# Moving PSUM copies of `ht` and `v` from VectorE to ScalarE in a two-layer graph network kernel

## The chip, the cores and the metric

The kernel runs on one core of one Trainium2 chip, as a single launch. The metric is device time in microseconds (us), as a median of several runs. A lower number is better. All data is float32.

## What is computed

The input `x` has 16 graphs of 1024 nodes and 256 channels; all graphs share one 1024 x 1024 adjacency matrix `adj`. Two layers follow each other, both with a layer norm and a ReLU ahead and a residual around them. Cut to what matters:

```python
# layer 0
h = max(layernorm(x), 0)
fea = h.transpose(0, 2, 1)                       # channels x nodes
diff = c_adj[:, None, :] - c_adj[:, :, None]     # c_adj: mean of h over channels
A_s = 2 * abs(abs(sigmoid(diff) - 0.5) - 0.5)    # symmetric
g = relu((fea @ (adj * A_s)) * para)             # the queries
k, v = split(h @ kv_w)                           # keys, values
x = x + softmax(q @ k.T * scale) @ v             # 4 heads of 64
# layer 1
h = max(layernorm(x), 0)
y = relu(batchnorm((A_hat @ h) @ W1.T + b1))     # A_hat: normalised adj + eye
x = x + batchnorm(y @ W2.T + b2)
```

The batch norms need statistics over all 16 graphs, so the second half of layer 1 starts only after the first half of the last graph.

## The kernel before

**Stages.** A short start prepares graph 0 (layer norm, transposes, keys, values, weights of the adjacency, queries). Then `attention()` runs over the graphs. While the attention of graph b is computed, a stream of smaller pieces called the background does other work: queries (`queries`), keys and values (`keys_values`) of graph b+1, the second layer norm and the product with the normalised adjacency for graph b-1 (`normed`, `aggregate`), the product with W1 for graph b-1 (`hidden`), and the layer norm and transposes for graph b+2 (`summed`, `prepare`). In the trace one graph takes about 146.75 us from about 192 us on. After the last graph, `second()` does the rest of layer 1.

**Order.** There is no automatic scheduling: the code issues instructions in the order in which it runs, and each engine executes its own list in that order. The list of one graph is 16 steps of attention (2 channel halves x 2 node halves x 4 pairs of key tiles). Each step issues two score products (line 882), their `exp` on ScalarE (line 890), one or more background pieces, and the products with the values for the step before (line 923). Background pieces have a cost in microseconds, and a piece is taken as long as the sum is behind its due value. `soon(...)` puts an action off to the next piece.

**The two places that the change touches.** `transposed(b, k)` turns the layer norm's output `h_a` (nodes x channels) into `ht` (channels x nodes): four TensorE transposes (line 396) fill one PSUM tile `htp` of 128 x 512, and one copy (line 399) brings it to SBUF. Two such tiles make one `ht`, and two `ht` one graph. `keys_values(b)` computes keys (`pk`, copied by ScalarE at line 624) and then values in four groups g: 16 matmul instructions fill one PSUM tile `pv`, and two copies of 128 x 256 (line 641) bring it to the two `v` tiles.

**PSUM tiles.** All these products take their tile from one pool with two buffers:

```python
ps_mm = st.enter_context(tc.tile_pool(name=f"ps_mm_{kind}", bufs=2, space=PSUM))
def bank(name):
    return ps_mm.tile([P, FB], F32, tag="mm", name=name)
```

So the third tile in a row can be written only when the first has been emptied: `pv` group 2 waits for the copies of group 0, and the product after a pair of `htp` tiles waits for the copy of the first of them. The score tiles `sc` have two buffers of their own, which `exp` empties.

**What stands around these copies.** On VectorE: the sums of the softmax (`acc`, lines 909 and 912), turning and folding them (lines 940 and 941), the weighting with `adj` (line 437), differences of the weights (line 512), combinations of the queries' products (lines 520 to 546), the scaling by `para` (line 498), statistics of the layer norms (line 317) and of the batch norm (line 741). On ScalarE: `exp` (line 890), `abs` and `tanh` for the weights (lines 450 and 458), ReLU of the queries (line 500, which waits for line 498) and of the layer norms (line 341), the copies of `o` (line 932) and of the first products (lines 515, 516, 673), and the bias for `y` (line 737).

Of the kernel before, what the change touches and what calls it, by code (L numbers as in the profile page):

```python
# [23 lines left out]
def gnn_two_layers_kernel(  # L24
# [12 lines left out]
    nc = tc.nc  # L37
# [6 lines left out]
    FB = 512  # L44
# [51 lines left out]
    def layers(shifted):  # L96
# [67 lines left out]
        def bank(name):  # L164
            return ps_mm.tile([P, FB], F32, tag="mm", name=name)

        def product(dst, left, right, start, stop):

            for e in range(2):
                r = slice(e * HW, (e + 1) * HW)  # L170
                nc.tensor.matmul(dst[r], left[:, r], right, start=start, stop=stop)  # L171
# [213 lines left out]
        def transposed(b, k, halves=range(NH)):  # L385

            h = hs["a", b]
            if 0 in halves:
                ht = p3.tile([P, N], F32, tag="ht", name=f"ht_{b}_{k}")
                hts.setdefault(b, []).append(ht)  # L390
            ht = hts[b][k]
            for g in halves:
                pt = bank(f"htp_{b}_{k}_{g}")
                for j in range(FB // P):
                    t = g * (FB // P) + j
                    nc.tensor.transpose(
                        pt[:, j * P : (j + 1) * P], h[:, t, k * P : (k + 1) * P], ident
                    )
                nc.vector.tensor_copy(ht[:, g * FB : (g + 1) * FB], pt)  # L399

        def differences(b):

# [210 lines left out]
        def keys_values(b):  # L613
            ht = hts[b]
            ks[b] = [p4.tile([P, N], F32, tag="k", name=f"k_{b}_{k}") for k in range(CC)]
            for g in range(NH):
                for j in range(CC):
                    cols = slice(g * FB, (g + 1) * FB)
                    pk = bank(f"pk_{b}_{j}_{g}")
                    for k in range(CC):  # L620
                        product(
                            pk, kvw[:, k, j * P : (j + 1) * P], ht[k][:, cols], k == 0, k == CC - 1
                        )
                    nc.scalar.copy(ks[b][j][:, cols], pk)  # L624
                    yield 1.71

            vs[b] = [p4.tile([P, NT, P], F32, tag="v", name=f"v_{b}_{k}") for k in range(CC)]
            for g in range(NT // 2):
                pv = bank(f"pv_{b}_{g}").rearrange("p (j c) -> p j c", j=2)
                for j in range(2):  # L630
                    t = 2 * g + j
                    for k in range(CC):
                        product(
                            pv[:, j, :],
                            ht[k][:, t * P : (t + 1) * P],
                            kvw[:, k, C : 2 * C],
                            k == 0,
                            k == CC - 1,
                        )
                for k in range(CC):  # L640
                    nc.vector.tensor_copy(  # L641
                        vs[b][k][:, 2 * g : 2 * g + 2, :], pv[:, :, k * P : (k + 1) * P]
                    )
                yield 1.71
# [127 lines left out]
        def prepare(b, products):  # L772


            yield from islice(products, 1)
            w = weighers[b]
            for k in range(CC):
                yield from weave(islice(products, 3), (0, islice(w, AHEAD // 2)))
                yield TOP
                transposed(b, k)  # L780
                yield 1.0
            yield from products
# [3 lines left out]
        def background(b):  # L786

            if b == 0:
                differences(1)
                for k in range(CC):  # L790
                    yield TOP
                    transposed(1, k)
                    yield 1.0
                w, products, norm = weighers[1], keys_values(1), Norm(2, True).all()
                yield from weave(
                    islice(products, 4), (0, double(islice(w, 8))), (0, islice(norm, 4))
                )
                yield from weave(
                    plain_queries(1), (0, norm), (0, w), (5, graph()), (7, degrees())
                )  # L800
                differences(2)
                yield from islice(products, 2)
                yield from prepare(2, products)
                return
            before = hidden(b - 1)
            gather = aggregate(b - 1)
            if b + 1 < B:
                w, products, norm = weighers[b + 1], keys_values(b + 1), normed(b - 1)
                yield from weave(islice(products, 4), (0, islice(w, 4)))
                if b == 1:  # L810
                    load_later()
                yield from weave(queries(b + 1), (0, double(w)), (9, islice(norm, 5)))
                yield next(gather)
                yield from weave(products, (0, norm))
            else:
                yield from weave(endings.pop(), (2, normed(b - 1)))
                yield next(gather)
# [240 lines left out]
        with st:  # L1058
            if shifted:
                for b in range(B):  # L1060
                    if b > 0:
                        load_x(b)
                    run(Norm(b, True).all())
                    differences(b)
                    for k in range(CC):
                        transposed(b, k)
                    run(islice(weighers[b], AHEAD))
                    run(weave(plain_queries(b), (0, weighers[b])))
                    if b == 0:
                        run(degrees(), graph())  # L1070
                        load_later()
                    run(keys_values(b))
                    shifted_attention(b)
                    norm = Norm(b, False)
                    run(norm.all())
                    nc.gpsimd.dma_start(out=x1_d[b], in_=xs[b])
                    if b == B - 1:
                        attn.close()
                        turns.append(second(kind))
                    run(aggregate(b), hidden(b))  # L1080
# [351 lines left out]
```

## Time and profile before

| | |
|---|---|
| median of three runs | 2658.61 us (2658.59 to 2659.17) |
| the profiled execution's own time | 2658.52 us |
| its span in the trace | 2656.6 us |
| TensorE (PE) matmuls busy | 2550.8 us, 96% of the span |
| VectorE (DVE) busy | 1904.3 us, 72% |
| ScalarE (ACT) busy | 1402.4 us, 53% |
| copies `ht<-htp` on VectorE, line 399 | 64 of 128x512, 40.6 us together |
| copies `v<-pv` on VectorE, line 641 | 128 of 128x256, 48.1 us together |

Busy time of an engine is the sum of its instructions in the trace. A matmul's busy time gets longer when the granted clock of TensorE is lower. A line of the waits names who waited, and which instruction ended the wait. A line of the timeline gives the start, the length, the engine, the line of the kernel, what is written and read, and in brackets the idle time of the engine just before, with what ended it. Times are counted from the start of the span.

### The profile page before, as it was taken

How to read it: one execution, taken by the hardware profiler on the slowest of the kernel's cores; microseconds unless marked ns; L12 is line 12 of the kernel's file. 1: busy time of each engine (PE TensorE's matmuls, PEld its weight loads, DVE VectorE, ACT ScalarE, POOL GpSimd, SP SyncE). 2: the span in 40 equal slices, each digit the busy share in tenths (PEclk: the TensorE clock that was granted, in tenths of full speed). 3: DMA queues.
4: the chain of work that ended last, by engine and by line, in shares of the span. 5: the costliest groups of instructions: out<-in, count | busy, mean ns of one | idle time of the engine just before them, and what ended most of it. 6: DMA issues, size and time to landing. Idle time of an engine off the chain costs nothing.

```text
span 2656.6 us, 31371 instructions
## 1 busy us (share of the span) xinstructions
PE 2550.8 (96%) x11626; PEld 948.2 (36%) x11626; DVE 1904.3 (72%) x3029; ACT 1402.4 (53%) x1841; POOL 391.4 (15%) x456
## 2 busy tenths in 40 slices
PE   8999999999999999999999999999999999989995
PEld 3333333333333333333333333333333333334443
DVE  5678686868777676868677686778686776657675
ACT  5774555646373645546463736455464734335544
POOL 1640001000000001000000000010000001026653
PEclk9999999999999999999999999999999999999997
DMA  4554333142524333341525243332415242355459
GB/s 165 182 180 170 100 107 136 59 175 72 178 83 148 105 138 100 103 140 58 184 76 178 80 151 99 132 111 95 144 60 183 80 147 103 112 189 211 185 188 368
DMA packets 131041, 363.45 MB, mean 137 GB/s; under 512 B 15424, under 2 KB 32320, under 8 KB 124736
## 3 DMA queue, kind: packets, MB, share of 16 engines
q1 hardware_dynamic: 110272, 282.70, 31.4%
q0 software_dynamic: 20608, 78.66, 7.8%
q8 instruction: 94, 1.54, 0.3%
q14 instruction: 67, 0.55, 0.1%
HBM read 286.79 MB, written 74.51 MB: 136 GB/s over the span
## 4 chain that ended last, share of the span: by engine, by line
PE 63%; DVE 21%; ACT 8%; issue 3%; DMA 2%; POOL 1%; SPq 0%; POOLq 0%; DVEq 0%; ACTq 0%
PE pa L171 14%; PE sc L882 12%; PE o L923 11%; PE m_f L1227 7%; PE py L171 7%; DVE acc L912 5%; PE pk L171 4%; ACT w L450 4%; DVE w L512 3%; PE pv L171 3%; PE pg L171 2%; DMA out_dram<-xo_f 2%; DVE w L437 2%; DVE st_b L317 1%; ACT w L458 1%
## 5 line engine op out<-in xcount | busy, mean ns | idle before, releaser
L890 ACT ACTIVATE p<-sc 128x1024 f32<-128x1024 f32 x512 | 494.8, 1019 | 484.3 <-PE sc L882 483.9
L912 DVE TENSOR_TENSOR acc<-acc,p 128x1024 f32<-128x1024 f32 x384 | 471.5, 1228 | 113.5 <-ACT p L890 92.2
L882 PE MATMUL sc<-q,k 64*128 64x512 f32 x2048 | 511.6, 618 | 3.3 <-ACT p L890 3.2
L923 PE MATMUL o<-p,v 128*64 128x512 f32 x2048 | 496.6, 606 | 0.0
L171 PE MATMUL pg<-w,h_a 128*64 128x512 f32 x1600 | 358.1, 592 | 3.7 <-ACT k L624 1.9
L171 PE MATMUL pa<-aht,h_b 128*64 128x512 f32 x1536 | 344.8, 593 | 3.5 <-ACT h_b L341 3.4
L882 PEld LDWEIGHTS sc<-q,k 64*128 64x128 f32 x2048 | 177.1, 187 | 330.2 <-issue 291.7
L450 ACT ACTIVATE w<-cbc,csum 128x512 f32<-128x512 f32 x256 | 293.7, 1199 | 0.0
L171 PE MATMUL py<-at,w 128*64 128x512 f32 x1024 | 232.3, 596 | 3.6 <-DVE ht L399 3.6
L437 DVE SCALAR_TENSOR_TENSOR w<-w,adj 128x1024 f32<-128x1024 f32 x128 | 159.6, 1247 | 78.3 <-ACT w L458 74.2
L923 PEld LDWEIGHTS o<-p,v 128*64 128x64 f32 x2048 | 124.3, 136 | 251.5 <-issue 248.4
L171 PEld LDWEIGHTS pg<-w,h_a 128*64 128x64 f32 x1600 | 115.5, 137 | 231.9 <-issue 213.7
L171 PEld LDWEIGHTS pa<-aht,h_b 128*64 128x64 f32 x1536 | 110.8, 137 | 216.9 <-issue 207.2
L738 POOL DMA_DIRECT2D y_d<-y x128 | 70.5, 551 | 788.9 <-ACT y L737 781.0
L737 ACT ACTIVATE y<-py,vec 128x512 f32<-128x512 f32 x128 | 87.5, 684 | 160.0 <-PE py L171 137.4
L171 PE MATMUL pv<-kvw_f,ht 128*64 128x256 f32 x1024 | 138.2, 424 | 34.0 <-DVE v L641 34.0
L458 ACT ACTIVATE w<-w 128x1024 f32<-128x1024 f32 x128 | 135.1, 1055 | 1.8
L741 DVE BATCH_NORM_STATS2 stats<-y 128x6 f32<-128x512 f32 x128 | 85.7, 688 | 69.7 <-ACT y L737 69.6
L512 DVE TENSOR_TENSOR w<-w,w 128x1024 f32<-128x1024 f32 x112 | 132.8, 1217 | 1.5
L93 POOL TENSOR_SCALAR lnsm_b<-mv_b 128x4 f32<-128x4 f32 x32 | 12.1, 379 | 793.4 <-DVE mv_b L319 793.4
L171 PEld LDWEIGHTS py<-at,w 128*64 128x64 f32 x1024 | 73.4, 138 | 153.8 <-issue 133.7
L341 ACT ACTIVATE h_b<-x,lnsm_b 128x256 f32<-128x256 f32 x128 | 67.8, 591 | 110.7 <-DVE lnsm_b L330 110.7
(155 smaller groups left out, 2806.9 us busy)
## 6 DMA issues: line engine op xcount, KB each, us to landing
aht<-aht_d SPq DMA_DIRECT2D x224, 512.0 KB, 5.6
adj<-in_adj_dram SPq DMA_DIRECT2D x128, 512.0 KB, 4.6
y_d<-y POOLq DMA_DIRECT2D x128, 256.0 KB, 2.6
yin_f<-y_d SPq DMA_DIRECT2D x32, 1024.0 KB, 6.3
x<-in_x_dram SPq DMA_DIRECT2D x32, 512.0 KB, 5.0
para<-in_para_dram SPq DMA_DIRECT2D x64, 256.0 KB, 3.9
x_d<-x POOLq DMA_DIRECT2D x16, 1024.0 KB, 10.4
xo_f<-x_d SPq DMA_DIRECT2D x32, 512.0 KB, 8.2
```

Source lines behind the costliest of these rows:

```text
L171: nc.tensor.matmul(dst[r], left[:, r], right, start=start, stop=stop)
L437: nc.vector.scalar_tensor_tensor(w, w, 1.0, a, op0=ALU.add, op1=ALU.mult)
L450: nc.scalar.activation(w[:, t, :].rearrange("p (t q) -> p t q", q=P), cbc[:, q * NT // NH : (q + 1) * NT // NH], AF.Abs, bias=csum[:, th * ...
L458: nc.scalar.activation(made[i], made[i], AF.Tanh, scale=-0.5 / C)
L512: nc.vector.tensor_sub(block(i)[part], block(x)[part], block(y)[part])
L737: nc.scalar.activation(y, made, AF.Identity, bias=b1[:, j : j + 1])
L741: nc.vector.bn_stats(stats1[:, j, i, :], y)
L882: nc.tensor.matmul(sc[:, e, :], ks[b][k][r, m * P : (m + 1) * P], qs[b][k][r, f * FB : (f + 1) * FB], start=True, stop=True,)
L890: nc.scalar.activation(pr, sc, AF.Exp)
L912: nc.vector.tensor_add(self.acc, self.acc, pr)
L923: nc.tensor.matmul(self.o[r, :], vs[b][k][:, m, r], pr[:, e, :], start=(m == 0), stop=(m == NT - 1),)
L1227: nc.tensor.matmul(made, left[:, j, :], right[:, j, :], start=(j == 0), stop=(j == JH - 1))
```

## The change

Both copies are issued on ScalarE in place of VectorE. Nothing else is edited: the places in the code, the tiles and their shapes stay. Since each engine's list follows the order of the code, each copy now stands in ScalarE's list at the point where the code reaches it.

```diff
@@ transposed @@
                     nc.tensor.transpose(
                         pt[:, j * P : (j + 1) * P], h[:, t, k * P : (k + 1) * P], ident
                     )
-                nc.vector.tensor_copy(ht[:, g * FB : (g + 1) * FB], pt)
+                nc.scalar.copy(ht[:, g * FB : (g + 1) * FB], pt)
@@ keys_values @@
                 for k in range(CC):
-                    nc.vector.tensor_copy(
+                    nc.scalar.copy(
                         vs[b][k][:, 2 * g : 2 * g + 2, :], pv[:, :, k * P : (k + 1) * P]
                     )
                 yield 1.71
```

## The prediction

> **What bounds the kernel now.** I read the busy shares first, then the waits of TensorE (PE), then the timeline around the longest of them, then the granted clock there.
>
> ```profile
> PE 2550.8 (96%) x11626; PEld 948.2 (36%) x11626; DVE 1904.3 (72%) x3029; ACT 1402.4 (53%) x1841; POOL 391.4 (15%) x456
> PE pv L171 <- DVE v L641: 34.0, 14, 2.6
> PE py L171 <- DVE ht L399: 3.6, 13, 0.3
> 1113.64 3.62 PE L171 MATMUL pv<-kvw_f,ht 128*64 128x256 f32 x32
> 1119.85 3.63 PE L171 MATMUL pv<-kvw_f,ht 128*64 128x256 f32 x16 [2.58 <-DVE v L641]
> 1127.44 1.90 PE L171 MATMUL pv<-kvw_f,ht 128*64 128x256 f32 x16
> ...
> core 0: us, PE busy (x), PEclk, DMA share, GB/s
> 1117.30:1119.80 2.50, 0.00 (x0) 1.00 0.97 239
> 1119.80:1123.40 3.60, 3.55 (x16) 0.53 1.00 419
> 1123.40:1125.30 1.90, 1.90 (x10) 1.00 1.00 401
> ```
>
> TensorE sets the pace: in a graph of 146.75 us it is busy 143.9 and waits 2.86, of which 2.58 is one wait, for the copies of `pv` group 0. The lines show a second cost that no wait names. After the gap the clock is 0.53 and 16 matmuls take 3.63 us; the same 16 take 1.90 at 1127. So busy time holds about 1.7 us per graph that the gap caused. The wait itself comes from VectorE's order:
>
> ```profile
> 1115.89 0.69 DVE L941 TENSOR_REDUCE part<-acc 128x16 f32<-128x512 f32 x1
> 1116.49 2.54 DVE L912 TENSOR_TENSOR acc<-acc,p 128x1024 f32<-128x1024 f32 x2
> 1118.95 0.75 DVE L641 COPY v<-pv 128x256 f32<-128x256 f32 x2
> ...
> 1114.52 1.92 ACT L890 ACTIVATE p<-sc 128x1024 f32<-128x1024 f32 x2
> 1116.32 2.07 ACT L341 ACTIVATE h_b<-x,lnsm_b 128x256 f32<-128x256 f32 x4
> 1120.34 0.63 ACT L500 ACTIVATE q<-q 128x512 f32<-128x512 f32 x1 [1.95 <-DVE q L498]
> ```
>
> Group 0 is full about 1115.4, halfway through the 32 matmuls, yet its copies start at 1118.95, behind turning, folding and the sums; VectorE has had no idle stretch over half a microsecond since 1080. ScalarE has gaps there.
>
> [...]
>
> **The parts, for one graph in the steady state.**
>
> *Durations.* ScalarE's copy of 128x512 from PSUM takes 580 ns (line 624, 64 of them), the next starts about 475 ns later. For 128x256 the trace has none; [...] a pair about 0.63 us (start to start 0.26). At most it costs like 128x512: a pair 1.05 us. I take 0.63. VectorE pays 419 ns and 674 ns (lines 641 and 399) now. All 192 copies move; ScalarE gains about 128 x 0.26 + 64 x 0.475 = 64 us, 4 us a graph on the 78.7 that it is busy. VectorE loses the 48.1 and 40.6 us of its two rows. No DMA and no semaphore queue moves: SP and POOL keep their lists.
>
> *Values.* In the code's order ScalarE's list reads: two `exp`, group 0, two ReLUs of `h_b`, group 1, two ReLUs, the ReLU of `q` (L500), group 2, two ReLUs, two `exp`, group 3. The first `exp` pair ends 1116.44, so group 0 is out at about 1117.0, while TensorE gets to group 2 at 1117.26 less its drain. With 0.15 us from copy to matmul (1119.70 to 1119.85 now) the wait is about 0.1, at the upper price 0.5. Group 1 is out by 1118.6 and is needed by TensorE only about 1123. Group 2 stands behind L500, which waits for VectorE until 1119.65; it is out about 1121, and the first `pa` product needs that buffer at about 1124.9. Saved: 2.57 - 0.1 = 2.47 in 13 graphs, 0.4 in the last: 32.5 us. The other copies are hidden in ScalarE's idle stretches of 1.95 us ahead of 1120.34 and 2.70 ahead of 1124.65; without these a pair would push the `exp` behind it by 0.63.
>
> *Clock.* Short gaps do not slow the trace: after 1.70 us at 49.17 and 1.88 us at 83.53 the matmuls run at full speed; after 2.29 us at 94.98 they do not (2.98 for 1.99). So with 0.1 us the drop goes: 12 graphs x 1.71 us (half of 3.41) = 20.5 us. The gap at 241.26 caused none, hence 12 and not 13.
>
> *Transposes.*
>
> ```profile
> 1040.60 1.91 ACT L890 ACTIVATE p<-sc 128x1024 f32<-128x1024 f32 x2
> 1042.05 1.28 DVE L399 COPY ht<-htp 128x512 f32<-128x512 f32 x2
> 1042.79 5.37 PE L171 MATMUL py<-at,w 128*64 128x512 f32 x24 [0.28 <-DVE ht L399]
> ```
>
> The code puts both pairs right behind two `exp`. At the first, ScalarE is late with these (an `abs` pair stands ahead), so the copy ends at about 1043.0 and `py` starts about 1043.15: 0.36 us later than now. At the second the `exp` run 1050.84 to 1052.76; the copy ends at 1053.25, and the next `py`, at 1053.02 now without a wait, begins 0.35 later. Lost: 13 x 0.71 = 9 us; with slower release 16. Behind these copies on ScalarE stand `y` copies, which wait for TensorE anyway (2.26 and 2.19 us idle now), so nothing more is pushed.
>
> *Graph 0.* Here ScalarE works straight on after the values:
>
> ```profile
> 163.37 2.38 ACT L450 ACTIVATE w<-cbc,csum 128x512 f32<-128x512 f32 x2
> 164.00 1.90 PE L171 MATMUL pv<-kvw_f,ht 128*64 128x256 f32 x16
> ```
>
> Now group 3's copy stands ahead of that `abs` and waits for TensorE until 165.85. The chain of `abs`, `tanh`, `exp` and two transposes' copies to 179 starts 3.1 us late and has two pairs of copies of 1.05 us more. TensorE waits about 2.4 us for the sixth score tile's buffer and 2.0 at the next unit's (0.47 of that now): 3.9 us, and up to 1.7 more if the clock drops. I take 5, once, range 3 to 7.
>
> *Start.* The first `ht` copies come behind eight ReLUs (end 12.6), so keys start about 1.6 us late, of which the 1.21 us wait at 19.0 gives most back. The weights then wait for `adj` (DMA, 4.06 us at 41.57) as before. I take 0.5 lost, from -1 to 2.
>
> *What is late next.* The `pa` products come 4.2 us earlier against their transfers: the first two of `aht` land at about 1117.8 and 1120.2 (issue 1113.8 and 1114.3, 4.0 and 5.9 us), needed at 1124.9 and 1126.6. The remaining waits are 0.1 and 0.6 us.
>
> **Sum.** 32.5 + 20.5 - 9 - 5 - 0.5 = 38.5 us. The profiled execution took 2658.52 us (span 2656.6), within 0.1 of the median, so I forecast 2658.6 - 38.5 = about 2620. Its own range: worst ends 32.5 - 5 + 20.5 - 16 - 7 - 2 = 23, best about 45: 2613 to 2636.
>
> **Rivals.**
> 1. *The drop of the clock stays.* Group 0 gets out late, behind `exp` that wait for L500 and thus for VectorE, and a gap over about 2 us remains. For it: the `exp` at 1114.52 is late now, for that reason. Against: it ends 0.8 us before TensorE arrives. If the gap shrinks by 1 us only, 13 us come, less 14.5: 2660, no change; if it shrinks to 1.5 without the drop, 13.9 + 20.5 - 14.5 = 20: 2639.
> 2. *Slower: ScalarE holds TensorE up in every graph as in graph 0*, by the copies that wait for a product while `exp` for the score buffers stands behind them. Place: group 3's copies and those of the transposes. If each of 13 graphs lost 5 us there, 53 - 14.5 - 65: 2685. It decides from an extra wait of 53/14, about 3.8 us a graph. For it: ScalarE's list is full from 1060 to 1086. Against: no moved copy lies in that stretch, and behind group 3 ScalarE waits 6.23 us for `pa` now.
> 3. *Another resource takes the gain*: `aht` lands after TensorE wants it. It needs 4 us more than the transfers take now; then 2650 to 2658.
> 4. *The change doesn't do what it says* is excluded by the code: both are plain edits of the engine.
>
> **Numbers.** A measurement of this kernel can tell about 0.2% (5.3 us) from no change. Forecast 0.78; rival 1 0.12, half of it faster and half the same; rival 2 0.06; rival 3 0.04, split like rival 1. Faster 0.78 + 0.06 + 0.02 = 0.86, same 0.08, slower 0.06. The range takes in the own range and the milder part of rival 1: 2608 to 2640.
>
> **What would show it.** Right: no wait of `pv` over 0.5 us for `v`, no window of half clock at `pv`, a graph about 143.3 us long (146.75 - 2.47 - 1.71 + 0.71), `py` waiting 13 times each at two places for `ht` on ScalarE, some 8 us in all, and a late `abs` at about 166. Wrong: `pv` waiting for line 641 on ScalarE over 1 us, half clock in every graph, or score products waiting for `exp` in each graph.

## The result and the profile after

The changed kernel takes 2615.36 us in the median (2614.78 to 2615.76, four runs) beside 2658.6 us before; the ratio is 0.9837 with a 95% interval of 0.982 to 0.9854. That is 43.2 us less; 38.5 were forecast. The profiled execution has a span of 2613.6 us, 43.0 less than before. The time lies near the fast end of the forecast's own range, 2613 to 2636.

The page of the changed kernel, first part, and below it two lines of its waits of TensorE (who waited, for what: us in total, times, longest):

```profile
PE 2525.8 (97%) x11626; PEld 931.8 (36%) x11626; DVE 1824.7 (70%) x2837; ACT 1468.9 (56%) x2033; POOL 393.6 (15%) x456
```

```profile
PE sc L882 <- ACT p L890: 8.8, 5, 2.4
...
PE py L171 <- ACT ht L399: 7.1, 13, 0.6
```

The same 11626 matmuls are busy 25 us less, so part of the gain lies inside what had counted as work. The wait of `pv` for `v`, 34.0 us before, is not in the list at all. In its place stand a longer wait of `py` for the transposes (3.6 before) and more waits of the score products for `exp` (3.2 before). VectorE is busy 79.6 us less, ScalarE 66.5 more.

The timeline of TensorE in the changed kernel, at the values of the graph that the prediction looked at, and the windows around the same place (length, busy time, granted clock, DMA share, GB/s):

```profile
1096.68 5.35 PE L171 MATMUL pv<-kvw_f,ht 128*64 128x256 f32 x48
1101.96 1.99 PE L882 MATMUL sc<-q,k 64*128 64x512 f32 x8
```

```profile
core 0: us, PE busy (x), PEclk, DMA share, GB/s
1096.60:1100.20 3.60, 3.60 (x36) 1.00 0.69 232
1100.20:1102.00 1.80, 1.80 (x20) 1.00 0.86 221
```

Groups 0, 1 and 2 now run as one block of 48 in 5.35 us, with no gap, and the clock stays at 1.00. Before, the third group alone took 2.58 us of waiting and 3.63 of matmuls. ScalarE's timeline there:

```profile
1097.54 1.92 ACT L890 ACTIVATE p<-sc 128x1024 f32<-128x1024 f32 x2
1099.35 0.65 ACT L641 COPY v<-pv 128x256 f32<-128x256 f32 x2
```

Group 0's pair starts right behind the `exp` and ends at 1100.0, just ahead of TensorE's need for its buffer at about 1100.2. The stretches of the span, taken from the first product `pk` of one graph to that of the next in the timelines, say where the 43 us lie:

| stretch | before | after | difference |
|---|---|---|---|
| to the first `pk` in the attention of graph 0 | 73.34 | 73.87 | +0.5 |
| graph 0 | 107.19 | 111.19 | +4.0 |
| the next 13, each | 145.06, then 146.60 to 146.77 | 142.84 to 142.87 | -48.5 together |
| the rest | 570.5 | 571.5 | +1.0 |

The first row and the last differ by less than they scatter. Four kernels of the experiments (e3, e5, e6, e7) do the same work up to the first `pk` in the attention, and take 72.39 to 74.12 us for it; the rest lies between 569.1 and 572.2 us over all ten traces.

### The profile page after: what moved, and what is told of

Its sections match the earlier page's. It is cut to its first block, busy times and chain, and to the rows that moved or that the text cites. A ratio compares the mean times of both kernels' runs of the same rounds, so it can differ in the third digit from the quotient of the medians.

```text
span 2613.6 us, 31371 instructions
## 1 busy us (share of the span) xinstructions
PE 2525.8 (97%) x11626; PEld 931.8 (36%) x11626; DVE 1824.7 (70%) x2837; ACT 1468.9 (56%) x2033; POOL 393.6 (15%) x456
## 5 line engine op out<-in xcount | busy, mean ns | idle before, releaser
L171 PE MATMUL pk<-ht,kvw_f 128*64 128x512 f32 x512 | 116.8, 599 | 2.5 <-ACT ht L399 1.5
```

## The experiments

Two theories stood against each other. **A**: all of the gain comes from one wait per graph, for the copies of values group 0, and from the half clock that it sets off; the other 160 of the 192 copies bring nothing and cost a little. **B**: the gain comes from taking 88.7 us off VectorE, and so in proportion to what is moved (88.7 is the sum of the two rows of copies). Edits are shown against the kernel before. `b` is the graph, `g` the group of values.

### Only the values (e1)

```diff
                 for k in range(CC):
-                    nc.vector.tensor_copy(
+                    nc.scalar.copy(
                         vs[b][k][:, 2 * g : 2 * g + 2, :], pv[:, :, k * P : (k + 1) * P]
```

> Only the values' copies (line 641) go to ScalarE; those of ht stay on VectorE. Theory A (the gain is one wait of 2.58 us a graph for pv group 0 plus the 1.71 us of half clock that it sets off; the transposes' copies on ScalarE cost a little): no wait of pv, no half clock from 300 to 2100 us, py waits 0.28 us a graph, graph about 142.4 us, total 2606 to 2610, better than the whole change by 5 to 9 us. Rival B (the gain comes from taking 88.7 us off VectorE, in proportion): 48.1/88.7 of 43 us, 2635.

Measured: 2605.25 us (ratio 0.9803, 0.979 to 0.9816), a graph 142.27 us long, `py` waiting 3.6 us as before. The transposes on ScalarE had therefore cost some 10 us of what the values gained; 7.5 of these are 0.58 us in each of 13 graphs, and the single executions of e1 spread over 4.7 us (2603.7 to 2608.4). B's 2635 is out. The total came 0.75 us below the range given for A.

### Only the transposes (e2)

```diff
-                nc.vector.tensor_copy(ht[:, g * FB : (g + 1) * FB], pt)
+                nc.scalar.copy(ht[:, g * FB : (g + 1) * FB], pt)
```

> Only the transposes' copies (line 399) go to ScalarE. Theory A: the wait of 2.6 us for pv group 0 and the half clock stay, py waits about 0.8 us a graph at two places, graph 0 loses 1 to 2 us: 2660 to 2669, no better than before. Rival B: 40.6/88.7 of 43 us, 2639.

Measured: 2667.02 us (ratio 1.0035, 1.0021 to 1.0049): 41 us of VectorE's work are gone and the kernel is slower. This run also parts the wait from the clock. Its timeline of TensorE, `pv` group 2 in two graphs in succession:

```profile
687.95 3.42 PE L171 MATMUL pv<-kvw_f,ht 128*64 128x256 f32 x16 [2.55 <-DVE v L641]
...
835.04 1.95 PE L171 MATMUL pv<-kvw_f,ht 128*64 128x256 f32 x16 [2.55 <-DVE v L641]
```

The wait is 2.55 us in both (2.55 to 2.58 in 12 of the 13 graphs, 2.93 in the first). In the first the matmuls behind it are slow, in the second not. The ten graphs with half clock behind the wait are 147.1 to 147.7 us long, the three without it 145.6. So the fall of the clock costs about 1.7 us by itself: 147.29 beside 145.63.

### Only group 0 of the values (e3)

```diff
                 for k in range(CC):
-                    nc.vector.tensor_copy(
+                    (nc.scalar.copy if g == 0 else nc.vector.tensor_copy)(
                         vs[b][k][:, 2 * g : 2 * g + 2, :], pv[:, :, k * P : (k + 1) * P]
```

> Only the two copies of values group 0 (32 of the 192 copies moved) go to ScalarE; groups 1 to 3 and ht stay on VectorE. Theory A: the whole gain without the losses in graph 0 (group 3 ahead of the abs chain) and at the transposes: no wait of pv, no half clock, graph about 142.4 us, graph 0 at 107.2 us as before: 2602 to 2607, the fastest. Rival B: 13 us off VectorE of 88.7, so 2652. Rival C (group 1 on VectorE becomes the next wait, since VectorE gets to it only about 1120): some of the 2.58 us comes back in group 3, 2620 to 2640.

Measured: 2601.88 us (ratio 0.9789, 0.9776 to 0.9803), the fastest of all: 32 copies give 56 us, while the change's 192 give 43. A graph is 142.27 us long and graph 0 takes 107.17, as A said; the total is 0.1 us below the range given for A. Rival C asked whether group 1 on VectorE is the next wait. From the timeline of this kernel:

```profile
1088.54 5.35 PE L171 MATMUL pv<-kvw_f,ht 128*64 128x256 f32 x48
1097.84 1.90 PE L171 MATMUL pv<-kvw_f,ht 128*64 128x256 f32 x16
...
1094.44 1.41 DVE L641 COPY v<-pv 128x256 f32<-128x256 f32 x4
```

VectorE's copies of groups 1 and 2 end at 1095.85, and TensorE wants the next buffer 2 us later, since a step of attention stands between group 2 and group 3. Group 1 may be late; only group 0 may not.

### All but group 0 (e4)

```diff
                 for k in range(CC):
-                    nc.vector.tensor_copy(
+                    (nc.vector.tensor_copy if g == 0 else nc.scalar.copy)(
                         vs[b][k][:, 2 * g : 2 * g + 2, :], pv[:, :, k * P : (k + 1) * P]
...
-                nc.vector.tensor_copy(ht[:, g * FB : (g + 1) * FB], pt)
+                nc.scalar.copy(ht[:, g * FB : (g + 1) * FB], pt)
```

> The whole change, with only group 0 of the values left on VectorE (160 of the 192 copies move). Theory A: the wait of 2.6 us and the half clock are back in each graph, and the losses of the change stay: 2662 to 2675, slower than before. Rival B: 160 of 192 copies moved, most of the gain stays, about 2622.

Measured: 2667.24 us (ratio 1.0034, 1.0021 to 1.0047). From its waits:

```profile
PE pv L171 <- DVE v L641: 33.3, 13, 2.6
```

With 160 of 192 copies moved the old wait is whole again and nothing of the gain is left. Together with e3 this settles A against B.

### How long a gap lowers the clock (e5, e6, e7)

On top of e3, group 0's pair is made several times over in the values of graphs 2 to 15, which holds its buffer longer. For three times:

```diff
-                for k in range(CC):
+                for k in list(range(CC)) * (3 if g == 0 and b > 1 else 1):
```

> Base: only group 0 on ScalarE (2601.9 us, graph 142.27). For graphs 2 to 15 the pair of copies of group 0 is made three times in a row (the same values each time), so TensorE's buffer comes free later by two pairs, 0.55 to 0.8 us each. Theory A [...]: pv waits 1.0 to 1.6 us in 13 graphs, no half clock, a graph 143.3 to 143.9, total 2615 to 2622. Rival D (any wait at this place sets off half clock): 1.7 us more in each graph, 2637 to 2644.

> As the run before, with the pair four times: pv waits 1.6 to 2.4 us. This lies at the threshold that the trace before showed (1.88 us without, 2.29 us with a fall). Theory A: half clock in some graphs or none, a graph 143.9 to 144.7 without and 1.7 us more with it; total 2623 to 2655. Rival D: half clock in all 13, 2645 to 2656.

> As the two before, with the pair six times: pv waits 2.7 to 4.0 us. Theory A: the wait and, in most graphs, half clock for 3.41 us with its 1.7 us, as before the change; a graph 146.3 to 148; total 2650 to 2680. Rival E (the 1.7 us of slow matmuls is no matter of the gap but of something else of VectorE's copies): no slow matmuls, a graph 145 to 146.3, 2637 to 2654.

| pair made | wait of `pv`, longest | stretches of half clock at `pv` | a graph | total | ratio |
|---|---|---|---|---|---|
| once (e3) | none | none | 142.27 | 2601.88 | 0.9789 (0.9776 to 0.9803) |
| three times (e5) | 0.9 | none | 143.34 | 2617.11 | 0.984 (0.9824 to 0.9857) |
| four times (e6) | 1.4 | none | 143.9 | 2623.06 | 0.9869 (0.9853 to 0.9886) |
| six times (e7) | 3.2 | in all 13 graphs | 146.97 to 148.52 | 2668.88 | 1.004 (1.0026 to 1.0055) |

First a line from the timeline of TensorE in e6 (four times), then the same place in e7 (six times), then the windows of e7 at these matmuls:

```profile
1102.45 1.95 PE L171 MATMUL pv<-kvw_f,ht 128*64 128x256 f32 x16 [1.42 <-ACT v L641]
```

```profile
1126.90 3.68 PE L171 MATMUL pv<-kvw_f,ht 128*64 128x256 f32 x16 [3.15 <-DVE v L641]
```

```profile
core 0: us, PE busy (x), PEclk, DMA share, GB/s
1126.80:1130.50 3.70, 3.60 (x16) 0.50 1.01 423
1130.50:1133.60 3.10, 3.10 (x11) 0.62 0.56 219
```

A wait of 1.42 us leaves the matmuls at full speed (1.95); one of 3.15 is followed by half clock and 3.68. Between e6 and e7 a graph grows by 3.1 to 4.6 us, though the wait grows by 1.8. The windows are from one of the three longest graphs, of 148.5 us: the clock is at half for all of the first 3.70 us and, by an estimate from the mean of 0.62, for about 2.4 of the next 3.10.

Rival D (any wait lowers the clock) falls with e5 and e6. Rival E (the slow matmuls come from something else of VectorE's copies) is not settled by e7, because there too VectorE's copies end the wait. In e2 the same wait for the same copies came three times without slow matmuls; and in e1, whose values are all copied by ScalarE, slow matmuls follow a gap of 2.42 us that an `exp` of ScalarE ended:

```profile
175.84 2.99 PE L882 MATMUL sc<-q,k 64*128 64x512 f32 x8 [2.42 <-ACT p L890]
```

Eight such products take 1.99 to 2.05 at full speed. So E falls too.

Two sizes were missed. e5 and e6 waited less than given: an extra pair takes 0.55 us (four pairs take 2.30 us in e6, six 3.41 in e7), the low end of the 0.55 to 0.8 given, and the first pair is out before TensorE needs its buffer, in e6 by about 0.3 us (1100.10 + 0.65 beside 1097.42 + 3.62). So e6 did not reach the stretch between 1.88 and 2.29 us in which the forecast had put the limit. In e7 the wait was for VectorE's copies of group 1, where ScalarE's had been expected: ScalarE's twelve copies end at 1126.18, VectorE's pair at 1126.75, and the matmuls start at 1126.90. Why group 2 waited for that buffer stays open. The gap's effect can be read all the same.

### Groups 0 to 2 of the values (e8)

```diff
-                    nc.vector.tensor_copy(
+                    (nc.scalar.copy if g < 3 else nc.vector.tensor_copy)(
```

> Values groups 0 to 2 on ScalarE, group 3 and ht on VectorE. If group 3's place ahead of the abs chain is what costs graph 0 (theory A), graph 0 is back at 107.2 us (110.73 with all four groups on ScalarE) with no wait of 2.4 us for exp between 160 and 185 us, the later graphs stay at 142.27, and the total is 2601 to 2604. Rival F (any of the moved copies loads ScalarE's chain in graph 0): 109 us or more there, total 2604 to 2606.

Measured: 2603.05 us (ratio 0.9792, 0.9776 to 0.9809). Graph 0 takes 107.21 us, where it takes 110.73 with all four groups on ScalarE (e1), so group 3 alone costs graph 0 its 3.5 us (in e1's trace a wait of 2.42 us and the half clock behind it, the line shown above). Rival F, with 109 or more, is out. Later graphs take 142.27, as in e1: there no group but group 0 matters.

## Why the prediction was right

Its mechanism came as described: one wait a graph and the fall of the clock behind it went, and the losses stood at the places named. The two large terms are shown by experiments; the small ones were partly luck, as said below.

**The wait of the values.** Forecast: 2.47 of 2.57 us saved in 13 graphs. The wait is gone and the matmuls run as one block, so 2.58 a graph or 33.5 us were saved. The 0.4 us put down for the last graph were misplaced: that wait of 0.42 us stands at 29.55, in the start. The pair takes 0.65 us, where the author's estimate was 0.63; one copy takes 376 ns in the median. That the `exp` ahead would end early enough was the tight point: the pair ends some 0.2 us ahead of TensorE.

**The clock.** Forecast: 12 falls, 20.5 us. In the trace before, the record of the clock has these 12 between 300 and 2100 us, each 3.41 us long; in the trace after it has none from 200 to 2200 us. So rival 1 did not come. That the cost is apart from the wait is shown by e2, that the gap causes it by e5 to e7. What was read wrongly is the limit, taken by the length of the gap as between 1.88 and 2.29 us. At the place of 94.98 all ten kernels have a gap of 2.29 to 2.31 us, and only three of them (before, e1, e8) half clock behind it: there the 8 products take 2.98, 3.32 and 2.53 us, in the others 2.03 or 2.04. This did no harm, since the gap of the values went to nothing. The last section has more such gaps. The stretch of half clock at 94.98 is gone too; TensorE now waits 1.71 us more for `exp` right after it, so this brought nothing.

**The transposes.** Forecast: 0.71 us a graph, 9 us. In the changed kernel the first place reads:

```profile
1023.07 1.93 ACT L890 ACTIVATE p<-sc 128x1024 f32<-128x1024 f32 x2
1024.88 1.06 ACT L399 COPY ht<-htp 128x512 f32<-128x512 f32 x2
...
1025.51 5.37 PE L171 MATMUL py<-at,w 128*64 128x512 f32 x24 [0.54 <-ACT ht L399]
```

The wait grew from 0.28 to 0.54, by 0.26 and not 0.36. At the second place the distance from the start of the products with the values to `py` grew from 1.77 to 2.03. That is 0.52 a graph, 6.8 us; the graph with the transposes on VectorE (e1) is 0.58 shorter. The 0.15 us allowed from the end of a copy to the matmul was too much: the first copy ends at 1025.46, 0.05 ahead of `py`. The list of waits has the first place alone (13 waits, 7.1 us), where the forecast expected waits at both.

**Graph 0.** Forecast: 5 us by waits of 2.4 and 2.0. Measured 4.0, with

```profile
166.44 0.65 ACT L641 COPY v<-pv 128x256 f32<-128x256 f32 x2 [2.45 <-PE pv L171]
166.98 2.38 ACT L450 ACTIVATE w<-cbc,csum 128x512 f32<-128x512 f32 x2
...
173.65 2.04 PE L882 MATMUL sc<-q,k 64*128 64x512 f32 x8 [2.44 <-ACT p L890]
...
180.72 2.05 PE L882 MATMUL sc<-q,k 64*128 64x512 f32 x8 [1.93 <-ACT p L890]
```

ScalarE waits 2.45 us for group 3 with the `abs` of the next weights behind it, and TensorE pays when the `exp` come late. The allowance of 1.1 us for a fall of the clock was not needed, and that was luck: in e1 almost the same wait at the same place, 2.42 us, was followed by half clock.

**The start** lost 0.5 us, as forecast; with a scatter of 1.7 us there, this agreement says nothing. **What was late next**: no wait for `aht` appears among those of TensorE, so rival 3 did not come.

**The terms that were off.** The 13 graphs gained 48.5 us where 43.6 were forecast (32.1 + 20.5 - 9, without the misplaced 0.4). About 1.4 of the difference are the wait, which went whole, and 1.5 the transposes (7.5 by e1, where 9 were put down). The forecast also left out that a gap costs more than its wait even at full clock: e5's graph is 1.07 us longer than e3's with a wait of 0.85, e6's 1.62 longer with one of 1.40. That is 0.22 us more, or 2.8 in 13 graphs. A fall of the clock cost about 1.66 (e2) where 1.71 was put down, 0.6 the other way in 12 graphs. Together that makes 5.1 where 4.9 are to be explained; the parts come from different kernels, so this is as close as they go. One more us came from graph 0, and the 1 us lost after the last of these stretches, for which nothing had been put down, is within the scatter.

Rival 2 (ScalarE holding TensorE up in every graph as in graph 0) named a real mechanism, which stayed in graph 0: with group 3 on ScalarE (e1) or on VectorE (e8) a later graph takes the same 142.27 us. Its break-even was miscounted: 53/14 leaves out the other losses, and 38.5/13, about 3.0 us a graph, would have done.

## What to carry to other kernels

When a copy frees a buffer that a bound engine wants, look for the one copy of a row that is waited for, and for what stands ahead of it in its engine's list: here 32 copies carried the gain, and 160 others that went along took 13 us of it back. A copy that waited for its product (2.45 us in graph 0) held up the work behind it in ScalarE's list, so look also at what stands behind its new place, graph by graph. Here a gap of TensorE cost more than its length (2.55 us of waiting and 1.7 of slow matmuls in e2), and the slow matmuls are booked as busy time; compare the same matmuls with and without a gap ahead.

## What was not expected of the hardware

The same gap does not always lower the clock. In all of 13 graphs of e2 TensorE waited 2.55 us or more for the values; in 10 of them the 16 matmuls behind the wait took 2.62 to 3.63 us, in the other three 1.95, full speed. In e4, with waits of 2.56 to 2.58, they took 3.18 to 3.63 us in nine graphs and 1.95 in four; before the change, with 2.56 to 2.60, 3.28 to 3.63 in twelve and 1.95 in one. In the changed kernel TensorE waited 2.44 us at 173.65 and the following 8 products took 2.04, full speed.

Nor does the length of a gap alone tell it. Behind one of 2.10 us (e1, at 50.18) 56 matmuls took 13.93 us, where the same 56 take 12.24 behind 1.70 in the kernel before; behind one of 2.58 us (e4, at 1127.61) 16 took 1.95. No run was made to find out what decides between two like gaps. So the 20 us of this term do not follow from the wait alone: with about the same wait the clock fell in 12 of 13 graphs before the change, in 10 in e2 and in 9 in e4.

ScalarE's copies out of PSUM were a little shorter than VectorE's of the same shape: medians of 376 ns beside 418 for 128x256, and 602 beside 681 for 128x512.
